# Layer 2 of a graph network: multiply first and mix afterwards, by Strassen's scheme, with its norms spread over the next product

## The chip, the cores and the metric

One core of one Trainium2 chip. The metric is the device time of one execution in microseconds (us). "Period" below is the time from the start of layer 2 of one quad (four batch elements) to that of the next, read from the trace.

## The reference, cut to what matters

```python
# four layers, each x = layernorm(x + layer(x)); x is (128 batch, 128 nodes, 256), adj is (128, 128), all float32
def layer2(x, W, adj, bias):                 # W is (3, 256, 256)
    adj_0, adj_1, adj_2 = diag(diagonal(adj)), triu(adj, k=1), tril(adj, k=-1)
    h = einsum('bjf,kfo->kbjo', x, W)
    return adj_0 @ h[0] + adj_1 @ h[1] + adj_2 @ h[2] + bias
```

Layer 0 is graph attention over 512 edges (scores, softmax, aggregation), layer 1 three products with mixing by adj*adj, layer 3 two products with batch norms over the whole batch. The order "mix, then multiply" is open to the kernel, since both steps are linear.

## The kernel before

It keeps four layers of neighbouring quads in flight: one iteration runs layer 2 of quad a, layer 1 of quad c = a + 1, parts of layer 0 of later quads, the first product of layer 3 of quad a. Each engine works its own queue in the order in which the program issues it. Several products already use Strassen's scheme (in Winograd's form): seven block products in place of eight, with sums on VectorE, and copies of running sums on ScalarE. A bank, below, is one of the accumulators that TensorE writes and VectorE and ScalarE read. The code here is cut and simplified: allocations and reshapes are left out.

```python
class Seven:                                   # one 2x2 block product in seven
    def p1(self): self.y = ps("y"); self.mm(self.y, "A11", "B11", True); self.k1 = self.part(self.y, 0)
    def p5(self): self.z = ps("z"); self.mm(self.z, "S1", "T1", True)
    def p2(self): x = ps("x"); self.mm(x, "A12", "B21", True); self.out(0, 0, x, self.k1)
    def p6(self): self.mm(self.y, "S2", "T2", False); self.k2 = self.part(self.y, 1)
    def p7(self): self.mm(self.y, "S3", "T3", False); self.k3 = self.part(self.y, 2); self.out(1, 1, self.z, self.k3)
    def p4(self): self.mm(self.y, "A22", "T4", False); self.out(1, 0, self.y, None)
    def p3(self): self.mm(self.z, "S4", "B22", False); self.out(0, 1, self.z, self.k2)

def norm_root(pool, mv):                       # the one ScalarE step of a layer norm
    nc.scalar.activation(sd, mv[:, :, 1], AF.Sqrt, bias=eps)
def layer_norm(pool, r):
    mv = norm_stats(pool, r)                   # VectorE
    norm_apply(pool, r, mv, norm_root(pool, mv))   # VectorE: reciprocal, scale

def stage_e(k):                                # layer 2
    def mix(i):
        for dc in range(DC):
            nc.tensor.matmul(pm[:, dc], s.xr[:, i, dc * P:(dc + 1) * P], split_t, ...)   # both triangles
        nc.scalar.copy(ms[:, 1:3], pm)
        for dc in range(DC):
            nc.tensor.transpose(pt[:, dc, :], s.xr[:, i, dc * P:(dc + 1) * P], ident)
        nc.vector.tensor_mul(ms[:, 0], pt, diag_bc)
    def prod(i):
        # six matmuls of 256 columns into po; after every second element
        nc.vector.tensor_add(xj, s.xb[:, i - 1:i + 1, :], po)
    mix(0); mix(1); yield; prod(0); yield; mix(2); prod(1); yield
    mix(3); layer_norm(wk, s.xr[:, 0:2, :]); prod(2); yield
    prod(3); layer_norm(wk, s.xr[:, 2:4, :]); ...

def second(k, between):                        # layer 1's second product, unchanged, cut
    ...
    product(y, 0, "S3", T3); keep(u3, 0, "u3")          # ScalarE copies u out of the bank
    total(0, 1, 1, z, u3); relu(1, 0, 0); after(7)      # VectorE: h = z + u; relu on ScalarE
    ...
    product(y, 0, "A22", T4); relu(0, 1, 0, y[0]); after(10)
    product(z, 0, "S4", B22)                            # adds into the bank that total(0, 1, 1) reads
    ...

def iteration(k):                              # cut to the head
    for _ in range(3): next(parts, None)       # the rest of layer 2 of quad a
    score(e, 0); gather_last(e)                # three VectorE passes of 1.2 us
    for _ in parts: pass
    ...                                        # score(e, 1..3), values_in(g) at step 11 of:
    second(c, between)
```

## Time and profile before

| | before |
|---|---|
| median (lowest to highest), us | 3186.81 (3184.70 to 3188.15), 4 runs, all fast |
| TensorE, VectorE, ScalarE busy | 98%, 68%, 41% |
| period | 86.92 us, TensorE busy 86.92 |
| TensorE waits from 345 to 2700 us | 1.2 us |

A run counts as fast here when it lies within 1.5% of the fastest run of its kernel.

The last row of the table is waits of TensorE summed by what ended them. Its columns are the waiting engine, the result and line it was going to make, what it waited for, the sum, the number and the longest. Before the change, 2355 us hold this and no more:

```profile
engine line waited for: us in total, times, longest us
PE y L757 <- ACT m L761: 0.7, 1, 0.7
PE y L757 <- ACT ag L731: 0.3, 1, 0.3
PE z L757 <- DVE ag L189: 0.2, 1, 0.2
```

### The profile page before, as it was taken

Reading aid. Unit: us, or ns where it says so; the run is one execution under the profiler, and the core shown is the slowest. Engines: PE = TensorE matmul, PEld = TensorE weight load, DVE = VectorE, ACT = ScalarE, POOL = GpSimd, SP = SyncE. Lnnn points to the kernel's source line nnn. Section 1 sums busy time; section 2 is a strip of 40 time slices with the busy share of each in tenths; the row PEclk is TensorE's granted clock in tenths of the full one; section 3 lists DMA queues with packets and bytes.
Section 4 is the critical chain, followed back from the end, with each engine's and each line's share of the span. In section 5 each row is a group of like instructions: output and inputs, shape, how many; then the busy total and the mean of one; then the engine's idle time right before and its main releaser. Section 6 shows DMA issues by size and latency. Waiting matters only on the chain. (4 is left out here: it accounts for less than half of the span.)

```text
span 3185.3 us, 40933 instructions
## 1 busy us (share of the span) xinstructions
PE 3119.4 (98%) x15658; PEld 2570.6 (81%) x15658; DVE 2164.1 (68%) x4210; ACT 1311.6 (41%) x2357; POOL 649.1 (20%) x533
## 2 busy tenths in 40 slices
PE   8899999999999999999999999999999999999997
PEld 3688888888888888888888888888888888874444
DVE  7676666666666766666666666766666666437878
ACT  3334333333443434333343443434333343326668
POOL 3211122221221111122211211111122211001235
PEclk8999999999999999999999999999999999999999
DMA  7322333333333322333333333322333331005557
GB/s 249 93 84 77 93 106 100 106 100 94 107 106 87 106 90 74 97 106 100 106 99 94 107 106 87 104 90 77 97 106 100 106 92 42 21 27 198 172 200 262
DMA packets 117459, 340.12 MB, mean 107 GB/s; under 512 B 14864, under 2 KB 51600, under 8 KB 108944
## 3 DMA queue, kind: packets, MB, share of 16 engines
q0 software_dynamic: 44400, 147.35, 19.3%
q1 hardware_dynamic: 71104, 189.23, 16.5%
q8 instruction: 124, 2.03, 0.3%
q10 hardware_dynamic: 1760, 0.92, 0.1%
q14 instruction: 71, 0.58, 0.1%
HBM read 252.00 MB, written 85.46 MB: 106 GB/s over the span
## 5 line engine op out<-in xcount | busy, mean ns | idle before, releaser
L647 PE MATMUL p<-w,h 128*128 128x256 f32 x2048 | 463.2, 379 | 0.0
L566 PE MATMUL ph<-m,w 128*128 128x256 f32 x2048 | 463.0, 379 | 0.0
L647 PEld LDWEIGHTS p<-w,h 128*128 128x128 f32 x2048 | 389.0, 190 | 66.6 <-issue 8.1
L566 PEld LDWEIGHTS ph<-m,w 128*128 128x128 f32 x2048 | 386.8, 190 | 51.4
L332 POOL DMA_INDIRECT zs<-qd,src_idx x120 | 117.0, 975 | 1379.0 <-DMA qd<-qt 828.9
L566 PE MATMUL ph<-m,w_s 128*128 128x256 f32 x1536 | 352.4, 379 | 0.0
L697 PE MATMUL po<-l2w,ms 128*128 128x256 f32 x1536 | 347.5, 379 | 1.3 <-DVE ms L689 1.3
L566 PEld LDWEIGHTS ph<-m,w_s 128*128 128x128 f32 x1536 | 291.9, 190 | 39.6
L697 PEld LDWEIGHTS po<-l2w,ms 128*128 128x128 f32 x1536 | 284.4, 190 | 36.1 <-DVE ms L689 1.5
L113 ACT ACTIVATE ln_sd<-ln_mv,eps 128x2 f32<-128x2 f32 x192 | 56.2, 293 | 498.8 <-DVE ln_mv L108 498.8
L332 POOL DMA_INDIRECT zs<-qd,dst_idx x120 | 204.2, 1702 | 246.7 <-DMA zs<-qd,src_idx 237.2
L414 POOL DMA_INDIRECT attd<-at,att_idx x128 | 127.8, 998 | 323.8 <-DMA attd<-at,att_idx 243.1
L573 ACT COPY u<-ph 128x512 f32<-128x512 f32 x128 | 74.9, 585 | 242.7 <-PE ph L566 242.7
L579 DVE TENSOR_TENSOR h<-ph,u 128x512 f32<-128x512 f32 x128 | 88.2, 689 | 105.1 <-ACT u L573 57.4
L366 DVE TENSOR_TENSOR zs<-zs,a_bc 128x1024 f32<-128x1024 f32 x125 | 153.1, 1225 | 4.3
L367 DVE TENSOR_REDUCE scores<-zs 128x16 f32<-128x1024 f32 x125 | 152.5, 1220 | 4.3
L685 ACT COPY ms<-pm 128x512 f32<-128x512 f32 x128 | 71.1, 580 | 200.0 <-PE pm L683 200.0
L364 DVE SCALAR_TENSOR_TENSOR zs<-zs 128x1024 f32<-128x1024 f32 x125 | 152.0, 1216 | 0.0
L508 DVE TENSOR_TENSOR h<-z,adc 128x512 f32<-128x512 f32 x62 | 41.8, 674 | 156.5 <-ACT adc L502 156.5
L106 DVE BATCH_NORM_STATS2 ln_st<-xr 128x6 f32<-128x256 f32 x384 | 144.2, 417 | 5.5
L121 DVE TENSOR_SCALAR xr<-xr,ln_mv,ln_rs 128x256 f32<-128x256 f32 x384 | 142.8, 414 | 6.9
L671 POOL TENSOR_TENSOR xb<-xr,bias 128x512 f32<-128x512 f32 x64 | 81.6, 1275 | 306.8 <-DVE xr L121 158.5
(304 smaller groups left out, 5705.5 us busy)
## 6 DMA issues: line engine op xcount, KB each, us to landing
ad<-attd SPq DMA_DIRECT2D x32, 1024.0 KB, 4.8
zd<-z SPq DMA_DIRECT2D x31, 1024.0 KB, 7.3
zl<-zd SPq DMA_DIRECT2D x62, 512.0 KB, 3.7
xr<-in_x_dram SPq DMA_DIRECT2D x32, 512.0 KB, 5.9
x3d<-xr SPq DMA_DIRECT2D x32, 512.0 KB, 3.0
x3l<-x3d SPq DMA_DIRECT2D x32, 512.0 KB, 4.9
out_dram<-x3l POOLq DMA_DIRECT2D x31, 512.0 KB, 4.6
qd<-qt SPq DMA_DIRECT2D x30, 512.0 KB, 2.6
```

What stands on the lines that cost most here:

```text
L106: nc.vector.bn_stats(st[:, i, :], r[:, i, :])
L121: nc.vector.tensor_scalar(r[:, i, :], r[:, i, :], mv[:, i, 0:1], rs[:, i:i + 1], op0=ALU.subtract, op1=ALU.mult)
L332: nc.gpsimd.indirect_dma_start(out=s.z[c], out_offset=None, in_=s.qd, in_offset=bass.IndirectOffsetOnAxis(ap=idx[:, c:c + 1], axis=0), com ...
L364: nc.vector.scalar_tensor_tensor(z, z, SLOPE, z, op0=ALU.mult, op1=ALU.max)
L366: nc.vector.tensor_mul(z3, z3, a_bc.unsqueeze(1).to_broadcast([P, QB, D]))
L367: nc.vector.reduce_sum(s.es[:, c, :], z.rearrange("p (r d) -> p r d", d=DH), axis=AX.X)
L414: nc.gpsimd.indirect_dma_start(out=ad, out_offset=bass.IndirectOffsetOnAxis(ap=att_idx[:, c:c + 1], axis=0), in_=s.at[:, c, :], in_offset= ...
L566: nc.tensor.matmul(bank[g][:, i].rearrange("p b n -> p (b n)"), wa[:, c, f:f + P], s.m2[:, blk_b, c].rearrange("p b n -> p (b n)"), start= ...
L579: nc.vector.tensor_add(block(g, row, col), bank[g], kept_[g])
L647: nc.tensor.matmul(p3[:, t * D:(t + 1) * D], s.h2[f // 2][:, f % 2, j + t, :], w3_sb[:, f, :], start=(f == 0), stop=(f == K2 - 1))
L671: nc.gpsimd.tensor_add(s.xb[:, j:j + 2, :], xj, bias.unsqueeze(1).to_broadcast([P, 2, D]))
L697: nc.tensor.matmul(po[:, i % 2, :], mss[i][:, t, dc, :], l2w[:, t, dc, :], start=(n3 == 0), stop=(n3 == 3 * DC - 1))
```

## The change

Its intent: less work for TensorE, which bounds the kernel. Two batch elements together are a 2x2 block matrix (two elements by two halves of the features) that is multiplied with the 256x768 weights in seven block products; the two triangles of adj are applied afterwards, the diagonal as one scaled addition on VectorE. The norms are taken apart (statistics in one step, root and scaling in a later one) and spread over layer 1's second product, and the first score goes to the end of the iteration before. Values for the queries move from step 11 to 13 (step n is the place after the n-th of the fourteen block products of `second`, counted from 0), and the start and iteration 0 are put in a new order.

```diff
-        def stage_e(k):
-            ...
+        def layer2(k, b):
+            def head(p):            # four transposes of a pair, ScalarE copies them
+            def products(p, xt):    # sums_a on VectorE, then Seven(mm, part, out), 384 columns each
+                def part(bank, i):
+                    nc.scalar.copy(to, bank[:, :half])
+                def out(row, col, bank, kept_):
+                    if kept_ is None: nc.scalar.copy(to, bank[:, :half])
+                    else: nc.vector.tensor_add(to, bank[:, :half], kept_)
+            def scaled(p):
+                nc.vector.scalar_tensor_tensor(xb, g[p][:, :, :D], diag_col, xb, op0=ALU.mult, op1=ALU.add)
+            def mix(p):             # two matmuls of 512 columns
+            def norm(p, po):
+                nc.vector.tensor_add(xj, s.xb[:, 2 * p:2 * p + 2, :], po)
+                return norm_stats(wk, xj)
+            def normed(p, mv):
+                norm_apply(wk, s.xr[:, 2 * p:2 * p + 2, :], mv, norm_root(wk, mv))
+            x0 = head(0)
+            yield
+            ...                     # u, v: the two pairs; layer 1's mixes of quad b between
+            run(u.p1, u.p2, u.p5, u.p6, v.p1, v.p2, u.p7, v.p5, v.p6, u.p4, u.p3, v.p7)
+            yield
+            scaled(0); v.p4()
+            yield
+            v.p3(); po = mix(0); scaled(1)
+            yield
+            mv = norm(0, po)
+            yield
+            po = mix(1)
+            yield
+            normed(0, mv); mv = norm(1, po)
+            yield
+            normed(1, mv)
 ... iteration(k)
-            for _ in range(3):
-                next(parts, None)
-            if has_e:
-                score(e, 0)
-                gather_last(e)
-            for _ in parts:
-                pass
+                for i in (0, 1, 2, 3, 5, 7):
+                    between[i].append(lambda: next(parts, None))
-                    for c_, i in enumerate((0, 2, 7)):
+                    for c_, i in enumerate((0, 3, 6)):
                         between[i].append(lambda c_=c_: score(e, c_ + 1))
-                    for j, i in enumerate((1, 3, 8, 10)):
+                    for j, i in enumerate((5, 8, 9, 10)):
                         between[i].append(lambda j=j: by_row(b, j))
-                    between[11].append(lambda: values_in(g, quads[g].xg))
+                    between[13].append(lambda: values_in(g, quads[g].xg))
 ... late in iteration(k)
+            if has_g:
+                score(g, 0)
+                gather_last(g)
 ... cut: buffers, a later load of w2, the new order of start() and iteration_0()
```

## The prediction

> **What bounds the kernel now.** I read the page's first two parts, then a table of windows cut at the repeat of one iteration, then the timeline of TensorE through layer 2, then the groups by line, and last the waits.
>
> ```profile
> PE 3119.4 (98%) x15658; PEld 2570.6 (81%) x15658; DVE 2164.1 (68%) x4210; ACT 1311.6 (41%) x2357; POOL 649.1 (20%) x533
> PE   8899999999999999999999999999999999999997
> ...
> PEclk8999999999999999999999999999999999999999
> ```
>
> TensorE is busy 98% of the span at full clock, from about 200 us on. Busy matmuls alone prove little, since their ends are modelled, so I cut the trace at the start of layer 2 of successive quads (four batch elements each):
>
> ```profile
> core 0: us, PE busy (x) PEld busy (x) DVE busy (x) ACT busy (x) POOL busy (x), PEclk, DMA share, GB/s
> 343.38:430.31 86.93, 86.93 (x463) 75.86 (x462) 59.36 (x114) 33.82 (x60) 16.90 (x14) 1.00 0.35 99
> 430.31:517.23 86.92, 86.92 (x462) 75.86 (x461) 59.03 (x114) 33.81 (x60) 17.14 (x14) 1.00 0.34 96
> ```
>
> The period repeats to 0.01 us and holds no idle TensorE; VectorE has 28 us free in each, ScalarE 53. The starts of successive matmuls therefore give their true price. Layer 2 of one quad:
>
> ```profile
> 517.23 1.02 PE L683 MATMUL pm<-split_t,xr 128*128 128x256 f32 x4
> 518.09 0.38 PE L688 MATMUL pt<-ident,xr 128*128 128x128 f32 x2
> 518.31 1.03 PE L683 MATMUL pm<-split_t,xr 128*128 128x256 f32 x4
> ...
> 519.40 3.74 PE L529 MATMUL pm<-wt_t,h 128*128 128x128 f32 x32
> 522.97 2.75 PE L697 MATMUL po<-l2w,ms 128*128 128x256 f32 x12
> 525.56 1.03 PE L683 MATMUL pm<-split_t,xr 128*128 128x256 f32 x4
> ...
> 535.50 5.34 PE L566 MATMUL ph<-m,w 128*128 128x256 f32 x24
> ```
>
> The reader should use starts, not durations: four records with 256 columns take 518.09 - 517.23 = 0.86 us, so 0.216 us each (one fp32 matmul is two records), two transposes 0.22 us. L529 in the middle belongs to layer 1 of the next quad. Layer 2 costs (519.40 - 517.23) + (535.50 - 522.97) = 14.70 us of TensorE a quad.
>
> **What the Trainium skill says.** "TensorE: Matmul & The Clock Gate", section "Back-to-back issue gap", gives N/2.4 + 2.5 ns for a warm matmul of N columns. "FP8 and Floating Point Precision", section "TensorE Precision Notes", says that true fp32 takes four passes. The trace agrees if each of the two records streams its columns twice: 512/2.4 + 2.5 = 215.8 ns against 0.216 us measured, and for 512 columns 429 ns against 0.43 us (502.42 to 503.28 for the two records of L660). So a record with 384 columns, which the old kernel has none of, should take 768/2.4 + 2.5 = 322.5 ns (estimate from both). "VectorE: DVE Perf Modes", section "The TRN2 errata — SBUF-src ops pay a fixed extra latency per instruction", gives (N+151)/0.96 ns for an fp32 tensor_tensor: 424 ns at 256 and 691 at 512, against 0.42 and 0.68 to 0.69 us here, also from PSUM. I take 0.29 us for 128 columns and 0.56 for 384. "ScalarE: Activation LUTs", section "What ACT_TABLE_LOAD costs", has 1283 ns for a table load, as here; the program's listing has 66 loads before and after, so the moved roots add none.
>
> **The change, part by part.**
>
> TensorE, one quad. Removed: 8 mixing matmuls and 24 product matmuls of 256 columns (64 records of 0.216 = 13.82 us). The 8 transposes (0.108 us each) stay. Added: seven products for each pair of elements, 14 matmuls of 384 columns, 28 x 0.3225 = 9.03 us; and mixing afterwards, 4 matmuls of 512 columns, 8 x 0.43 = 3.44 us. New stage: 0.86 + 9.03 + 3.44 = 13.33 us. It saves 14.70 - 13.33 = 1.36 us a quad, 1.6% of the period. Plain multiplying first would have cost 16 matmuls of 384 in place of 14, 1.3 us more: nearly the whole gain is Strassen's missing eighth product.
>
> The other engines, one quad.
>
> ```profile
> L685 ACT COPY ms<-pm 128x512 f32<-128x512 f32 x128 | 71.1, 580 | 200.0 <-PE pm L683 200.0
> L689 DVE TENSOR_TENSOR ms<-pt,diag_bc 128x256 f32<-128x256 f32 x128 | 51.1, 419 | 49.9 <-PE pt L688 49.9
> ```
>
> VectorE loses the four L689 multiplies (-1.7 us) and gains 8 block sums of 128 columns (2.3), 6 additions of 384 out of PSUM (3.3) and 2 scaled additions of 512 (1.4): +5.3 us, to about 64 of 85.6. ScalarE loses four copies of 0.58 and gains two of 512 and eight of 384 columns (about 0.48 each): +2.7 us, to 37. Neither becomes the bound on average. This work costs time only where TensorE, which runs in order, waits for it.
>
> So I followed one iteration in the order listing of the changed program, with the durations above. The score moved a stage earlier (three VectorE passes, 3.66 us) lands here:
>
> ```profile
> 509.60 0.69 DVE L508 TENSOR_TENSOR h<-x,adc 128x512 f32<-128x512 f32 x1 [2.13 <-PE x L288]
> 515.38 0.69 DVE L508 TENSOR_TENSOR h<-z,adc 128x512 f32<-128x512 f32 x1 [5.09 <-ACT adc L502]
> ```
>
> VectorE sits idle 5.09 us there, so the move is free and takes as much from the crowded stretch after layer 2. Take the first new transpose as 0. TensorE has it, three layer-1 mixes, the second transposes at 3.1 us. Those need the norm: layer 1's last ReLU, the copy of the first transposes and the root stand in ScalarE's queue, then two VectorE scalings end near 3.4, so I charge 0.1 us there. The first product starts at 4.6. The products' needs then come in time: the second pair's sums at about 6.2 for use at 9.1; the bank of z freed at 10.5 for use at 11.1; only the last product before layer 1's multiplication waits on a copy by a few hundredths. The two products left over are put between blocks of the next multiplication, and the second mix needs a result of about 20.0 at 22.2. The norms end near 36 and are first read after 41. I find 0.1 to 0.15 us of new waiting, so 1.25 net, 31 times: 39 us.
>
> The last quad has nothing to stand beside.
>
> ```profile
> 2836.62 1.02 PE L683 MATMUL pm<-split_t,xr 128*128 128x256 f32 x4
> ...
> 2852.83 1.05 PE L728 MATMUL pa<-ahat_t,xr 128*128 128x128 f32 x8
> 2855.82 1.26 PE L728 MATMUL pa<-ahat_t,xr 128*128 128x128 f32 x8 [1.94 <-DVE xr L121]
> ```
>
> Before, the second half of the next stage starts 19.2 us after this stage begins. Now both mixes come after all products, and both norms (about 3.3 us each through VectorE and ScalarE) follow each other after that; my sum is 21.4. That loses 2 us.
>
> The start: TensorE idles about 20 us in the first 100 and 5 in the next 75. A matmul that spread the diagonal, with its 3.04 us wait, is gone. Copies that waited 3.30 us behind a softmax now come before it, and the last score is no longer waited for before aggregation. Against this, setting up the new weight blocks and an early score crowd iteration 0, where I expect 1 to 3 us of waiting. I take -5 us net, the loosest term.
>
> Sum: 3187 - 39 + 2 - 5 = 3145 us, a ratio of 0.987.
>
> **The rivals.**
>
> First, *TensorE comes to wait on VectorE every iteration*. The six additions free the banks that the products need, in a stretch where VectorE has little rest; seven-product chains also pass through ScalarE copies of the running sum three times a pair. For it: my margins are 0.5 to 3 us, and one late VectorE instruction would shift everything behind it. Against it: three other seven-product stages already run here with waits near zero. 0.5 us an iteration would give 3157, 1.3 us nothing gained, 3186.
>
> Second, *fewer weight loads pay too*. The stage loads weights for 36 records in place of 64, apart from the transposes. If loads of 190 ns slow the records they stand beside, the gain is more than columns tell. Against it: 256-column records already go at the 215.8 ns of columns alone, so loads are hidden. It would give at most a few us, 3135 to 3140.
>
> Third, *the start gains more*. If most of the 25 us idle at the start go, the time is about 3130. Some of it (5.2 us for the first input, the dependent scans of softmax) cannot go.
>
> A fourth, that the late load of the last layer's weights is waited for, I hold to be nothing: it is issued more than three iterations before use and DMA is a third busy.
>
> **Range and chances.** The 39 us follow from counts and repeatable durations and I trust them to 3 us if TensorE stays fed; the start is good to 5 us either way, and rival one could take 15. So 3131 to 3162, with the longer arm above. Faster by over 2% needs under 3123, 22 us beyond my sum with no source for them: 0.03. Slower by over 2% needs TensorE starved by 3.3 us an iteration: 0.02.
>
> **What would show it.** Right: periods near 85.7 us with TensorE at 100%; records of the products 0.322 us apart; VectorE about 64 us a period; the score in the former gap; no TensorE wait in the middle above a few tenths; the last quad some 2 us longer. Wrong: a period of 86.3 or more with TensorE waits on L723 additions or L715 copies (rival one); records under 0.32 us apart (rival two); under 10 us idle in the first 175 us (rival three).

## The result, and the profile after

The changed kernel took 3204.43 us (3201.54 to 3207.12, 4 runs, all fast) against 3186.81: a ratio of 1.0056, with the interval 1.0038 to 1.0073. Ratios here are the mean time of one kernel's fast runs over that of the other's fast runs of the same rounds, so not quite the ratio of the medians quoted. The kernel became 0.6% slower where 1.3% faster was predicted; the time lies outside the predicted range.

First the page's totals and its slices:

```profile
PE 3105.5 (97%) x14760; PEld 2407.4 (75%) x14760; DVE 2301.8 (72%) x4598; ACT 1392.7 (44%) x2549; POOL 646.2 (20%) x533
...
PE   7999999999999999999999999999999999989998
```

TensorE has 898 records fewer, as counted, yet the page still says 97%. Only the table of windows, cut at the starts of layer 2, shows that something is off:

```profile
435.55:522.91 87.36, 86.42 (x434) 70.56 (x433) 63.30 (x126) 36.34 (x66) 16.62 (x14) 1.00 0.34 97
```

The columns are the window, its length, then busy time and records of TensorE, weight loads, VectorE, ScalarE and GpSimd. The period is 87.36 us where 86.92 was before, and TensorE idles 0.94 us of it. The TensorE waits from 345 to 2700 us name the two causes (the others come to 2.9 us):

```profile
PE z L289 <- DVE m L181: 12.7, 26, 0.5
PE ph L571 <- DVE h L584: 11.1, 27, 0.4
```

Both recur once per period. The stage itself costs what was predicted: in the timeline of TensorE its products (two records each) start 0.64 to 0.65 us apart.

```profile
440.09 0.81 PE L708 MATMUL y<-l2w,x2t 128*128 128x384 f32 x2
440.74 0.81 PE L708 MATMUL x<-l2w,x2t 128*128 128x384 f32 x2
441.38 0.81 PE L708 MATMUL z<-l2w,adc 128*128 128x384 f32 x2
```

The two waits in the same timeline, 36.6 and 46.5 us after layer 2 began at 435.55:

```profile
468.10 3.62 PE L571 MATMUL ph<-m,w 128*128 128x256 f32 x16
472.12 1.99 PE L571 MATMUL ph<-m,w_s 128*128 128x256 f32 x8 [0.41 <-DVE h L584]
...
480.38 1.13 PE L289 MATMUL y<-wqv,xt 128*128 128x256 f32 x4
482.00 1.10 PE L289 MATMUL z<-wqv,m 128*128 128x256 f32 x4 [0.49 <-DVE m L181]
```

Sixteen records of 256 columns need 16 x 0.216 = 3.46 us, so the next could have started at 471.56; it started at 472.12, 0.56 later. It is the product S4 of layer 1, which adds into a bank that VectorE's sum for h (L584) must have read first. VectorE's queue up to that sum:

```profile
457.54 0.75 DVE L106 BATCH_NORM_STATS2 ln_st<-xr 128x6 f32<-128x256 f32 x2
458.21 0.30 DVE L108 BATCH_NORM_AGGREGATE ln_mv<-ln_st 128x2 f32<-128x6 f32 x2
...
464.45 0.17 DVE L119 RECIPROCAL ln_rs<-ln_sd 128x2 f32<-128x2 f32 x1 [2.31 <-ACT ln_sd L113]
...
467.48 1.22 DVE L365 SCALAR_TENSOR_TENSOR zs<-zs 128x1024 f32<-128x1024 f32 x1
...
471.38 0.68 DVE L584 TENSOR_TENSOR h<-ph,u 128x512 f32<-128x512 f32 x1
```

VectorE, with 24 us to spare in each period, stood still 2.31 us for the root of a norm, and the rest of its queue, a score and then the sum for h, came later. And ScalarE's queue ahead of that root:

```profile
461.39 0.58 ACT L578 COPY u<-ph 128x512 f32<-128x512 f32 x1 [8.67 <-PE ph L571]
463.12 0.58 ACT L578 COPY u<-ph 128x512 f32<-128x512 f32 x1 [1.14 <-PE ph L571]
463.60 0.63 ACT L588 ACTIVATE h<-h 128x512 f32<-128x512 f32 x1
464.13 0.29 ACT L113 ACTIVATE ln_sd<-ln_mv,eps 128x2 f32<-128x2 f32 x1
```

The statistics were done at 458.51 (458.21 + 0.30). ScalarE did nothing until 461.39, then two copies of u and a ReLU that stand ahead of the root, since `normed(0)` was issued after them. A root of 0.29 us began 5.6 us late because of what stood in front of it in a queue that is 44% busy.

Outside the steady iterations I compare landmarks of the two traces (before, after): first layer 2 at 169.53 and 172.05, so +2.5 us at the start; 28 periods, +14.5; the last three periods, which have no queries, -2.1; the last quad up to the second half of its aggregation 19.2 and 22.5, +3.3; all after that -3.7. That makes the 14.5 us between the two traced spans. The last quad after the change:

```profile
2851.52 0.60 PE L694 MATMUL pt<-ident,xr 128*128 128x128 f32 x4
...
2871.15 1.26 PE L790 MATMUL pa<-ahat_t,xr 128*128 128x128 f32 x8 [1.04 <-DVE xr L121]
2874.06 1.53 PE L790 MATMUL pa<-ahat_t,xr 128*128 128x128 f32 x8 [1.64 <-DVE xr L121]
```

### The profile page after: what moved, and what is told of

Same layout as the page of the kernel before. It is cut to its first block, busy times and chain, and to the rows that moved or that the text cites. A ratio compares the mean times of both kernels' runs of the same rounds, so it can differ in the third digit from the quotient of the medians.

```text
span 3199.8 us, 39789 instructions
## 1 busy us (share of the span) xinstructions
PE 3105.5 (97%) x14760; PEld 2407.4 (75%) x14760; DVE 2301.8 (72%) x4598; ACT 1392.7 (44%) x2549; POOL 646.2 (20%) x533
## 5 line engine op out<-in xcount | busy, mean ns | idle before, releaser
L571 PE MATMUL ph<-m,w 128*128 128x256 f32 x2048 | 473.1, 379 | 0.0
L571 PE MATMUL ph<-m,w_s 128*128 128x256 f32 x1536 | 360.5, 381 | 11.9 <-DVE h L584 11.9
L333 POOL DMA_INDIRECT zs<-qd,dst_idx x120 | 189.4, 1578 | 346.9 <-DMA zs<-qd,src_idx 338.3
L415 POOL DMA_INDIRECT attd<-at,att_idx x128 | 140.8, 1100 | 349.4 <-DMA attd<-at,att_idx 253.6
L588 ACT ACTIVATE h<-h 128x512 f32<-128x512 f32 x192 | 121.0, 630 | 118.1 <-DVE h L584 118.1
L715 ACT COPY x2k<-y 128x384 f32<-128x384 f32 x192 | 91.8, 478 | 141.1 <-PE y L708 113.5
L434 ACT COPY adc<-ad 128x512 f32<-128x512 f32 x126 | 134.9, 1071 | 8.3 <-DMA ad<-attd 8.3
L119 DVE RECIPROCAL ln_rs<-ln_sd 128x2 f32<-128x2 f32 x192 | 31.3, 163 | 148.0 <-ACT ln_sd L113 148.0
L676 POOL TENSOR_TENSOR xb<-xr,bias 128x512 f32<-128x512 f32 x64 | 99.1, 1548 | 168.3 <-DVE xr L121 150.8
L529 PE MATMUL pm<-wt_t,h 128*128 128x128 f32 x1024 | 128.8, 279 | 0.0
```

Of the source, the lines that this page charges most:

```text
L333: nc.gpsimd.indirect_dma_start(out=s.z[c], out_offset=None, in_=s.qd, in_offset=bass.IndirectOffsetOnAxis(ap=idx[:, c:c + 1], axis=0), com ...
L415: nc.gpsimd.indirect_dma_start(out=ad, out_offset=bass.IndirectOffsetOnAxis(ap=att_idx[:, c:c + 1], axis=0), in_=s.at[:, c, :], in_offset= ...
L434: (copy or nc.scalar.copy)(s.adc[:, j * H:(j + 1) * H, :], s.ad.rearrange("p (s r) -> p r s", r=R)[:, j * H:(j + 1) * H, :])
L529: nc.tensor.matmul(pm[:, c // 2, c % 2, :], quads[k].h1[i, c], wt_t, start=True, stop=True)
L571: nc.tensor.matmul(bank[g][:, i].rearrange("p b n -> p (b n)"), wa[:, c, f:f + P], s.m2[:, blk_b, c].rearrange("p b n -> p (b n)"), start= ...
L588: nc.scalar.activation(h, h if src_ is None else src_, AF.Relu)
```

## The experiments

Two theories. The **order theory**: TensorE's saving is real, and what ate it is the place of single instructions in the queues of ScalarE and VectorE, the late root first. The **load theory**: VectorE simply has too much to do around layer 2 (63.3 us of the period in place of 59), so lighter work for it would help and another place would not. Twelve kernels ran, all correct. Each group of four shared one chip and the runs of the kernel before, whose medians were 3188.58, 3190.51 and 3189.06 us.

**The root at once (e1_root).** The root is issued right after its statistics.

```diff
-                return norm_stats(wk, xj)
+                mv = norm_stats(wk, xj)
+                return mv, norm_root(wk, mv)
-                norm_apply(wk, s.xr[:, 2 * p:2 * p + 2, :], mv, norm_root(wk, mv))
+                norm_apply(wk, s.xr[:, 2 * p:2 * p + 2, :], *mv)
```

> The change with one edit: the square root of each layer-2 norm is issued to ScalarE right after the statistics, not next to the scaling two or three products later. Order theory (the loss comes from where instructions stand in the queues): VectorE's 2.31 us wait for the root at the first norm's reciprocal goes, and with it the 0.41 us TensorE wait for an addition before the last products of the first column (0.56 us by starts); the wait for the queries' block sums (about 0.97 by starts) stays or shrinks a little. Period 86.4 to 86.8 in place of 87.37, time 3174 to 3190. Load theory (VectorE simply has 5 us too much work a period, whatever the order): period 87.2 to 87.4, time 3200 to 3207.

Measured: 3153.48 us (3150.39 to 3161.64), ratio 0.9894 [0.9876, 0.9911]. One period of it:

```profile
427.77:513.52 85.75, 85.75 (x435) 70.58 (x433) 63.16 (x126) 36.45 (x66) 17.09 (x14) 1.00 0.35 99
```

VectorE has the same work in it, 63.16 us, and TensorE no idle time. From 345 to 2600 us TensorE waits 0.6 us in all. ScalarE and VectorE:

```profile
450.77 0.30 ACT L113 ACTIVATE ln_sd<-ln_mv,eps 128x2 f32<-128x2 f32 x1 [5.83 <-DVE ln_mv L108]
453.67 0.58 ACT L578 COPY u<-ph 128x512 f32<-128x512 f32 x1 [2.60 <-PE ph L571]
```

```profile
454.28 0.15 DVE L119 RECIPROCAL ln_rs<-ln_sd 128x2 f32<-128x2 f32 x1
...
461.58 0.68 DVE L584 TENSOR_TENSOR h<-ph,u 128x512 f32<-128x512 f32 x1
```

The root is done before the copies, the reciprocal does not wait, and the sum for h starts 33.8 us after layer 2's start where it was 35.8. I had expected the second wait to stay; it vanished too. It was a consequence: VectorE's first scan of the softmax starts 39.5 us after layer 2's start here and 41.1 in the changed kernel, and the copies and sums that the queries wait for stand behind the scans. Moving one step of 0.3 us is worth 51 us in the medians, which come from two different groups of runs, and 47.8 between the traced spans. Of these 45.6 lie in the 28 full periods, 1.6 in each; the remaining 2.2 are differences of the start, the end and the last periods.

**The values back at step 11 (e2_values), and both (e3_both).**

```diff
-                    between[13].append(lambda: values_in(g, quads[g].xg))
+                    between[11].append(lambda: values_in(g, quads[g].xg))
```

> The change with one edit: the transposes of the quad whose queries come next are put back two products earlier, where the kernel before had them. Order theory: TensorE's 0.49 us wait for the queries' block sums and the late copy before it go (0.97 us by starts), the wait at the last products of the first column stays at about 0.4; period about 86.4, time 3174 to 3182. Load theory: the two copies only enter VectorE's queue earlier and delay the additions there; period 87.1 to 87.4, time 3197 to 3207.

> Both edits together. Order theory: no TensorE wait over 0.1 us is left in the period, so 86.92 less the 1.3 us that the stage's records save plus a tenth or two: 85.7 to 85.9, time 3153 to 3165, faster than the kernel before by about 1%. Load theory: above 3195.

Measured: e2_values 3170.89 us (3169.56 to 3177.45), ratio 0.9942 [0.9925, 0.9959], period 86.33; e3_both 3153.38 us (3151.53 to 3155.82), ratio 0.9888 [0.9871, 0.9904], period 85.66. Moving the values takes 1.03 us off the period (e2_values came out somewhat faster than the 3174 to 3182 us expected): the second wait goes and the first stays (from 345 to 2600 us, 10.7 us in 26 times). With the early root it adds nothing to speak of. So the late values turn a delay into a second wait, but the delay itself comes from the root. e3_both is the base of later experiments.

**Less work for VectorE (e6_pool).** Two subtractions go to GpSimd, 1.4 us of VectorE's period.

```diff
-            nc.vector.tensor_sub(m2[T2], m2[B22], m2[T1])
-            nc.vector.tensor_sub(m2[T4], m2[B21], m2[T2])
+            nc.gpsimd.tensor_sub(m2[T2], m2[B22], m2[T1])
+            nc.gpsimd.tensor_sub(m2[T4], m2[B21], m2[T2])
```

> The change with 1.4 us a period of VectorE work taken away at the head of the crowded stretch: the two late block sums of layer 1 go to GpSimd, which is idle there; no order on ScalarE changes. Order theory: the root comes no sooner, VectorE only waits longer for it (3.7 in place of 2.31 us), so the period stays 87.2 to 87.4 and the time 3199 to 3207. Load theory: both TensorE waits shrink by most of their size; period 86.7 or less, time under 3190.

Measured: 3203.27 us (3201.69 to 3203.83), ratio 1.0043 [1.0026, 1.0060], with VectorE at 61.83 us and the period at 87.37, both waits unchanged (from 345 to 2600 us, where the changed kernel has 12.7 and 10.7):

```profile
PE z L289 <- DVE m L181: 12.8, 26, 0.5
PE ph L571 <- DVE h L584: 10.6, 26, 0.4
```

The load theory does not hold. The freed time became idle time: VectorE waits 1.69 us for TensorE ahead of the first sum for h, where it had waited 0.36, and then 2.32 us for the root as before (3.7 was expected); the sum for h that TensorE waits for starts 35.8 us after layer 2's start in both. This run alone would not refute the theory, since the work taken away lies ahead of the root, and no run lightened the work behind it. What refutes it is e1_root: the same 63.16 us of work, and no wait.

**One root at a time (e10_root0, e11_root1).** Both on the changed kernel:

```diff
+                return mv, norm_root(wk, mv) if p == 0 else None     # e11_root1: p == 1
...
+                norm_apply(wk, s.xr[:, 2 * p:2 * p + 2, :], mv, sd or norm_root(wk, mv))
```

> The changed kernel, with only the first pair's root in layer 2 issued right after its statistics; the second pair's stays where the change put it. Order theory, by the trace of the changed kernel: the first pair's root starts 5.6 us after its statistics are done, behind two copies that wait for TensorE, and VectorE waits 2.31 us for it; the second pair's starts 1.1 us after, and VectorE does not wait. So nearly the whole effect of e1_root: period 85.7 to 85.9 us, 3150 to 3160 us. If it is the sum of both roots that counts (each about half): period near 86.5, 3172 to 3182 us.

> The other half: only the second pair's root issued right after its statistics, the first pair's as in the changed kernel. Order theory: nothing, period 87.2 to 87.5 us, 3196 to 3208 us, both waits of TensorE (for h and for m) as in the changed kernel. If each root counts: period near 86.5, 3172 to 3182 us.

Measured: e10_root0 3154.98 us (3154.01 to 3155.86), ratio 0.9897 [0.9881, 0.9914], period 85.74; e11_root1 3203.21 us (3199.42 to 3207.17), ratio 1.0049 [1.0033, 1.0066], period 87.38 with both waits. The whole loss hangs on the first pair's root, the one for which VectorE waited 2.31 us. The second pair's root was late by 1.1 us, nobody waited for it, and moving it does nothing.

**The first score back at the head (e4_late),** on e3_both, undoing "first scores a stage sooner":

```diff
+            if has_e:
+                score(e, 0)
+                gather_last(e)
 ... and out at the end of the iteration:
-                score(g, 0)
-                gather_last(g)
```

> The version with the early root and the values in their old place (e3_both, 3153.4 us, period 85.67), with the first score and its gather back at the head of the iteration, as the kernel before had it: this undoes 'first scores a stage sooner'. Order theory (VectorE's queue right after the layer-2 stage is so full, with only 0.4 us idle in the 6 us ahead of the second product's first sum, that another 3.7 us of scoring there must push that sum and the norms back until TensorE waits): 0.3 to 1.5 us more per iteration, 3162 to 3200 us, with TensorE's wait for h (L584 or so) coming back. Load theory (the same VectorE work in the period whichever the place, about 64 of 86 us, so place means nothing): 3150 to 3157 us, no wait of TensorE over 2 us in all in the steady iterations.

Measured: 3188.80 us (3186.02 to 3189.81), ratio 0.9999 [0.9983, 1.0016]. A period, and the wait in it, from VectorE's and TensorE's timelines:

```profile
430.12:517.23 87.11, 86.03 (x434) 70.54 (x433) 63.80 (x126) 36.28 (x66) 17.25 (x14) 1.00 0.35 98
```

```profile
451.73 1.22 DVE L368 TENSOR_REDUCE scores<-zs 128x16 f32<-128x1024 f32 x1
452.86 0.55 DVE L723 TENSOR_TENSOR adc<-z,x2k 128x384 f32<-128x384 f32 x1
```

```profile
453.55 1.96 PE L734 MATMUL po<-adc,split_t 128*128 128x512 f32 x4 [1.08 <-DVE adc L723]
```

Two scores in a row now stand ahead of the addition that the second mix reads, and TensorE waits 1.08 us for it in every period; the period is 1.45 longer than in e3_both. So the early score is not decoration: without it the change, even with the early root, would gain nothing. The wait is for another line than I had named.

**Eight plain products (e5_plain),** on e3_both, to price Strassen's scheme itself:

```diff
-                return Seven(mm, part, out)
+                def block(row, col, copy):
+                    bank = ps("y")
+                    mm(bank, f"A{row + 1}1", f"B1{col + 1}", True)
+                    mm(bank, f"A{row + 1}2", f"B2{col + 1}", False)
+                    copy(g[p][:, row, col * half:(col + 1) * half], bank[:, :half])
+                return block
```

> e3_both with eight plain block products in place of the seven of Strassen's scheme, two accumulated per block, without the sums of blocks; multiplying first and mixing afterwards stays. If the seven products are worth what TensorE's records say (four more records of 0.3225 us per iteration, 1.29 us, while VectorE and ScalarE lose about 5 us of work each that lay beside it): period 86.95 us, 3186 to 3196 us, so about level with the kernel before; the whole gain is then the missing eighth product. If the scheme's additions and copies cost on the path what the eighth product costs, and the gain is in multiplying first: 3150 to 3165 us.

Measured: 3189.41 us (3187.76 to 3192.55), ratio 1.0002 [0.9986, 1.0019]:

```profile
434.10:521.04 86.94, 86.94 (x439) 71.46 (x437) 62.27 (x116) 34.51 (x62) 20.01 (x17) 1.00 0.36 102
```

The period is 86.94, that is 1.28 above e3_both, where four records of 0.3225 make 1.29. Multiplying first without the scheme is worth nothing against the kernel before (86.92); the gain is the missing eighth product.

**The tail, twice, and the start (e7_tail, e12_tail, e8_start), then all together (e13_best).** e7_tail runs all products of the last quad's first pair, then the second's with the first pair's mix and norm between; e12_tail also puts the second pair's transposes later. e8_start takes back the start's order of scores, values and mixes.

```diff
 e12_tail (e7_tail: head(1) before, u.p1 u.p5 u.p2 u.p6 u.p7 u.p4 u.p3 | v.p1 v.p5 v.p2 | mix(0) ...)
+            if b is None:
+                run(u.p1, u.p2, u.p5); x1 = head(1); v = products(1, x1)
+                run(u.p6, v.p1, u.p7, v.p2, u.p4, u.p3, v.p5); scaled(0); v.p6()
+                po = mix(0); mv = norm(0, po); v.p7(); normed(0, mv)
+                run(v.p4, v.p3); scaled(1); po = mix(1); mv = norm(1, po); normed(1, mv)
 e8_start, in start()
+            score(1, 0, ...)                     # again ahead of the mixing matrices
-            for i in range(QB): values(3, i, nc.scalar.copy)
+            values(3, 0, ...); ...; score(1, 2, ...); score(1, NE - 1, ...); values(3, 1..3, ...)
-            ... sorted_scores split in two, mix1 and first between softmax steps
+            ... sorted_scores whole, softmax steps, then mix1 and first
```

> e3_both with the last quadruple's layer 2, which has nothing to lie beside, put in another order: all seven products of the first pair, then those of the second with the first pair's mix and norm between them, then the second's mix and norm. If the 3.3 us that the last quadruple got longer by are waits for norms that stand one behind the other: 3 to 5 us less than e3_both, 3148 to 3151 us, with the stretch from the last quadruple's first transpose to the first aggregation's record near 20 us in place of 24. If they are work of TensorE that no order removes: within 1 us of e3_both.

> e3_both with the kernel before's order in the start (scores, values, mixes up to the first iteration), all else as in e3_both. If the new order of the start is what costs: 2 to 4 us less than e3_both, 3149 to 3152 us, the first aggregation again near 80.8 us and the first layer-2 stage 2 to 4 us earlier than in e3_both. If the start is bound by the first attention matrix's way through memory in both orders, and iteration 0's crowd on VectorE does the rest: within 1.5 us of e3_both.

> e3_both with the last quadruple's layer 2 in a second other order: the second pair's transposes, for which TensorE waited 2.5 us and then ran its next four products at nearly half speed, stand after the first pair's first three products; the rest interleaved, with the first pair's mix and norm between the second pair's last products. If the loss in the tail is that wait and the slow clock after it: from the last quadruple's first transpose to the first half of the aggregation 16 to 18 us in place of 19.8, 2 to 4 us off the time, near 3150 us. If it is the chain of norms at the end: no gain, within 1 us of e3_both.

> All that helped together: early root, values in their old place, the kernel before's start, and the second other order of the last quadruple. If the savings add: start 3.3 us and tail 2 to 4 us below e3_both, 3145 to 3149 us. If they do not (the tail gives nothing): near e8_start's 3151 us, 3149 to 3152.

| | median (range), us | ratio to before | first layer 2 at | last quad, us |
|---|---|---|---|---|
| e3_both | 3153.38 (3151.53 to 3155.82) | 0.9888 | 171.41 | 22.7 |
| e7_tail | 3153.92 (3151.36 to 3158.26) | 0.9896 | 169.56 | 23.3 |
| e8_start | 3151.06 (3148.17 to 3153.07) | 0.9886 | 168.12 | 21.0 |
| e12_tail | 3155.59 (3151.05 to 3156.66) | 0.9901 | 169.80 | 22.3 |
| e13_best | 3152.02 (3147.24 to 3156.95) | 0.9894 | 167.61 | 22.3 |

The last column is from the last quad's first transpose to the second half of its aggregation. With the change's own tail it takes one of two lengths from trace to trace: 21.0 us in e1_root, e6_pool, e8_start and e10_root0, 22.4 to 22.7 in e2_values, e3_both, e4_late, e11_root1 and the changed kernel. The traces show what separates them. TensorE waits 2.5 us for the second transposes in all nine, but in the five long ones its granted clock is 0.50 for some 3 us from about the end of that wait on (products 1.2 us a pair in e3_both in place of 0.65), and in the four short ones it stays at 1.00. Why the clock falls in some and not in others stays open. The traces of e7_tail, e12_tail and e13_best have the full clock there, so they are to be compared with 21.0: these orders lose 1.3 to 2.3 us in the one trace of each, and my expectation had taken a slow-clock tail for the rule. Both orders moved waits about. In e12_tail ScalarE shows how:

```profile
2812.75 0.48 ACT L715 COPY x2k<-y 128x384 f32<-128x384 f32 x1 [1.46 <-PE y L708]
2816.19 0.30 ACT L113 ACTIVATE ln_sd<-ln_mv,eps 128x2 f32<-128x2 f32 x1 [2.97 <-DVE ln_mv L108]
2816.39 0.46 ACT L715 COPY x2k<-y 128x384 f32<-128x384 f32 x1
```

Here the *early* root does the harm: it waits 2.97 us for its statistics, the copy of a running sum stands behind it, and TensorE waits 1.83 us for that copy. Right after the statistics is the right place only where nothing urgent is issued behind it.

In the trace of e8_start the first layer 2 begins 3.3 us sooner than in e3_both, and 2.6 us of this are there at the end of the first aggregation (L448: 82.36 and 79.76). The reason is TensorE's order ahead of it. First the changed kernel, whose wait is like that of e3_both (7.77 us), then e8_start:

```profile
71.57 0.59 PE L357 MATMUL pe<-w_s,scores 128*16 128x512 f32 x1
80.29 3.68 PE L448 MATMUL py<-adc,m 128*64 128x128 f32 x32 [8.12 <-ACT adc L434]
```

```profile
73.05 2.75 PE L357 MATMUL pe<-w_s,scores 128*16 128x512 f32 x6
76.24 1.03 PE L357 MATMUL pe<-w_s,scores 128*16 128x512 f32 x2 [0.44 <-DVE scores L370]
77.78 2.06 PE L448 MATMUL py<-adc,m 128*64 128x128 f32 x32 [0.51 <-ACT adc L434]
```

The new order had taken the work out from under the wait for the first attention matrix, which comes through memory: TensorE came to it 8 us early, idled, and then ran its 32 records in 3.68 us in place of 2.06, at a granted clock of 0.50 in place of 1.00. The gain of the old order must be read with care, since the start too varies from trace to trace: in nine traces with the new order the first layer 2 begins at 169.1 to 169.8 (five of them, with 5.4 to 6.7 us of that wait) or at 171.4 to 172.1 (four, with 7.8 to 8.3), with the old one at 168.1 and 167.6. (e4_late and e5_plain are not counted, since their iteration 0 differs.) So the old start is worth 1 to 4 us in the traces; in the medians 2 us do not stand out of ranges that overlap. e13_best adds nothing to e8_start. The best versions are e8_start and e3_both, 1.1% below the kernel before.

A second cost of the start is in every trace with the change but one: in iteration 0 TensorE waits 2.8 us for a sum for h that stands on VectorE behind the early score. In e3_both:

```profile
169.55 2.07 PE L289 MATMUL z<-w,adc 128*128 128x256 f32 x4 [2.84 <-DVE h L509]
```

e4_late, which has no score there, has no such wait, and its first layer 2 begins at 167.38 in spite of the new order. No run takes out that one score alone.

## Why the prediction was wrong, point by point

**TensorE's work** was right. The stage took 13.36 us by starts for 13.33 predicted. (The saving written there as 14.70 - 13.33 = 1.36 is 1.37.) With no waits (e3_both) the period is 85.66, where 86.92 less 1.36 is 85.56; the tenth left over does not show as a wait of TensorE. e5_plain put the eighth product at 1.28 us for 1.29.

**VectorE's and ScalarE's loads** were right in size for ScalarE (36.3 for 37) and VectorE (63.3 for about 64). That neither would be the bound was right, and the conclusion "this work costs time only where TensorE, which runs in order, waits for it" too.

**The step that failed is "I find 0.1 to 0.15 us of new waiting".** Measured: 1.7 us a period (87.36 against 85.66 without the waits), of which 0.94 shows as idle TensorE and the rest as longer records next to the waits. In the walk through the iteration I charged the roots of layer 1's norm, but for those of layer 2 I wrote only that "the norms end near 36 and are first read after 41". That was nearly true (the second is scaled by 37.4 us after the start, and first read at 42.8) and beside the point: what matters is not who reads the norm but what stands behind its waiting reciprocal in VectorE's queue. The Trainium skill states the premise: "TensorE: Matmul & The Clock Gate", section "Architectural detail: the array is 16× 32×32, not 1× 128×128", has ScalarE and VectorE as strictly first in, first out. The trace agrees: the reciprocal waited 2.31 us, and a score and the sum for h that needed nothing from it started only afterwards; e10_root0 alone took the loss away, e11_root1 did not. The sum of predicted terms should thus have had about +1.6 us a period in place of +0.1, some 50 us, where e1_root measured 51 in the medians and 47.8 between the traces.

**Rival one** (TensorE comes to wait on VectorE, 1.3 us an iteration and nothing gained) is what happened. I had put it at up to 15 us and looked for it in the banks of layer 2's own products (L723, L715). Those were waited for once from 345 to 2700 us, 0.6 us for L715 (three times in e3_both); the waits that cost the time came 36 and 46 us after the stage began, in layer 1 and layer 0. Only e4_late shows the rival in the line it was given, L723. **Rival two** is refused by the product starts of 0.64 to 0.65 us a pair, those of columns alone. **Rival three** is refused by the start: TensorE idled 27.4 us in the first 175, where it had been 25.4. The fourth, the late load of the last layer's weights, was indeed nothing: no TensorE wait after 2600 us names that load.

**The early score** landed where it was said to, and "takes as much from the crowded stretch" was right: e4_late makes it worth 1.45 us a period. (VectorE's gap there shrank from 5.09 to 1.45 us.)

**The start**, -5 us, "the loosest term", was wrong: +2.5 us in the trace compared, -0.4 to +2.5 over the nine traces with this start. I had counted waits that the change removed, and not that the work moved had lain under a wait that stays, 8.12 us for the first attention matrix. The early score in iteration 0, allowed for with 1 to 3 us of waiting, made one wait of 2.8. **The last quad**, +2 us, was right for the full clock: 21.0 us in place of 19.2 (21.4 predicted). The trace compared had +3.3, since its clock fell to 0.50. Why the clock falls there in some traces, and why the first attention matrix is waited for 5.4 us in some and 8.3 in others, stays open. The -3.7 us after the last quad were not predicted; that stretch takes 324.4 to 330.0 us over the traces of the variants, so they lie within what varies from trace to trace.

With the early root in place the terms compare like this, from the traces of e3_both and before: start +1.9 (predicted -5), 31 iterations -34.3 (-39; nearly all of the 28 full periods are 1.26 shorter than before, but the first of e3_both is 2.3 longer than the others, and three more are 0.9 longer, each with one wait of 0.6 to 0.7 us for an L715 copy), last quad +3.5 (+2), the rest -3.3 (0).

## What to carry to other kernels

When a stage is spread over another's instructions, follow the queues of the helping engines too, one by one: for each instruction that will wait, ask what stands behind it, and whether TensorE needs that. A tiny step on a half-idle engine (a root of 0.29 us) can cost a hundred times its size over a kernel if it is issued behind copies that wait for TensorE; issue it where its input is ready and nothing urgent stands behind it. If a change that saves work does not save time, compare busy with length in one period before blaming the new load.

## What the Trainium skill lacked or had wrong

- "TensorE: Matmul & The Clock Gate", section "Back-to-back issue gap": its gap formula does not say how a float32 matmul fits in. Here it is two records, each at the gap of twice its columns: 0.216 us for 256, 0.322 for 384, 0.43 for 512.
- "TensorE: Matmul & The Clock Gate", the strict queues of ScalarE and VectorE: it does not say what they cost. One root of 0.29 us behind two copies cost 1.6 us a period, 51 us of 3204; one issued too early held a copy and TensorE for 1.83 us.
- No page has a case of Strassen's scheme: the product that it saves was worth 1.28 us of 1.29 counted per period with the queues in order (e3_both against e5_plain), and none of it reached the time in the changed kernel as it stood (ratio 1.0056).
